# A convolutional transformer block: centre tap as the unit, and no zero padding in the depthwise convolution

## The chip, the cores and the metric

The kernel runs on one core of one Trainium2 chip. The metric is the device time of one execution in microseconds. The kernel before took 4169.58 us, the median of three runs from 4163.44 to 4169.85.

## The reference

The input x has 16 images of 128 channels and 96 x 96 pixels, in float32. One block is computed, cut here to what matters:

```
xn1 = layernorm(x)                       # over the channels of a pixel
x   = x + (attention(xn1 wq, wk, wv) @ wp)   # 8 heads, attention over channels, softmax of 16 x 16
xn2 = layernorm(x)
h1  = w_in . xn2                         # 1x1 projection, 128 -> 512 channels
h2  = depthwise 3x3 conv of h1, padding 1    # one 3x3 filter per channel
x   = x + w_out . gelu(h2)               # 1x1 projection, 512 -> 128 channels
```

The padding is what the change is about: at the image's border a tap of the 3x3 filter meets zeros.

## The kernel before

**Tiles.** The 128 channels lie on the 128 partitions. An image is worked in 8 bands of 12 rows (BR) and a band in 3 units of 4 rows (UR, 384 pixels). There are 128 bands in all. The 512 hidden channels are 4 chunks of 128. TensorE (PE), VectorE (DVE), ScalarE (ACT) and GpSimd (POOL) all work on the convolution; SyncE (SP) issues loads and stores.

**Two ways through the convolution.** Chunks 0 to 2 of every band, and chunk 3 of 62 bands, are "jobs" (conv_job, 446 of them). In a job, PE projects the normalised rows (hidden, L901), ACT copies the result from PSUM into the padded buffer h1s (kept, L906), DVE adds most of the taps (tap, L919: h3 = h1 shifted x ratio + what was there), and ACT makes the products of two or three taps (product, L914), which POOL's accumulating DMAs add up (add_products, L923). Then ACT applies gelu (L927). For chunk 3 of the other 66 bands (by_pe: every second band, which always includes an image's last band, and six of the last eight bands) projection and convolution are one: nine matmuls with composed weights comp, one for each tap, accumulate into one bank (by_matmuls, L969). At the end four matmuls of a unit apply w_out (ffn_out, L992), DVE adds the result to x (L999), and SP stores the band (L1003).

**The unit weight.** The scalar weight of tap 0 is folded into the projection (units, unit_parts), so tap 0 has weight 1. The other taps have the weight divided by it (ratio). DVE's first tap takes the unweighted tap 0 as its second operand, and so does two taps in one instruction.

**Padding.** The rows of the buffers xns (24 rows and two more) and h1s (12 and two more) have WP = 97 columns: one column of zeros serves as the right border of a row and the left border of the next. `window(t, r, n, dx)` is n rows of 96 columns from row r and column dx on. `zeros` fills the border columns of all six xns and four h1s once (L395, L396); `ends` zeroes, for every image, the row above the first and the one below the last (L408). In an image's first band `hidden` projects the zero row above too, in the last band the one below, so that h1s holds zeros there. A job of a later band takes its two upper rows over from the band before (halo, L897), except chunk 3. Chunks of rows are 5, 5, 4 without the halo and 4, 4, 4 with it. So every tap of a job works on 12 x 96 = 1152 elements, and every tap matmul on 384 columns.

**Taps.** Tap t is row t // 3, column t % 3 of the filter; its shift is dy, dx = divmod(t, 3). DMA_TAPS = (1, 2, 3): taps 1 and 2 of each job go over the DMA adds; tap 3 as well for chunk 1. The last job of all has none. DVE has the rest.

**Order.** The instructions' order is written out ahead of time by a planner (class Plan): every step has an engine, a place and dependencies, and an engine always takes the ready step with the smallest place. A place is a job's number plus an offset from the table AT (`at(kind, place)`), with offsets of their own for image 0 (`..._0`). Steps whose offsets differ by more than a few jobs have in effect a fixed rank on their engine.

Of the kernel before, what the change touches and what calls it, by code (L numbers as in the profile page):

```python
# [11 lines left out]
ALU = mybir.AluOpType  # L12
# [5 lines left out]
UR = 4  # L18
BR = 12
# [3 lines left out]
PE_LAST = (0, 1, 2, 4, 5, 7)  # L23
TINY = 1e-20
UNIT_MIN = 1e-18
DMA_TAPS = (1, 2, 3)
THIRD, THIRD_OF, THIRD_CHUNK = (0, 1, 2), 3, 1
PART, Z_PARTS = 24, 6
QT, QB = 4, 1
# [1 line left out]
X1_BUFS, XB_BUFS, PR_BUFS, H3_BUFS, ZT_BUFS = 2, 6, 5, 10, 3  # L31
IN_TURN = ("tr", "h3", "pr", "xb", "x1")
AT = dict(
    load_w=-10.6, weights=-9.25, zeros=-109.85, load_a=-167.55, forth_a=-12.1, stats_a=-7.7, variance_a=338.3,
    power_a=317.55, scaled_a=106.3, gram=-0.45, back_a=-56.1, place_a=121.25, attention=-165.9, mix=-18.8,
    residual=290.95, mixed=-105.85, add_x=-328.55, forth_b=-9.7, stats_b=-262.9, variance_b=95.55,
    power_b=-203.35, shift_b=-87.55, scaled_b=78.75, back_b=0.45, place_b=-79.8, halo=240.1, hidden=4.1,
    kept=-109.5, products=36.25, add_last=-62.55, tap=5.55, add_first=-157.75, gelu=210.35, conv=3.8,
    conv_gelu=5.25, out=7.35, add=0.7, store=226.8, mix_0=-63.1, residual_0=490.65, mixed_0=-265.75,
    add_x_0=-380.65, gram_0=43.45, forth_a_0=-198.65, forth_b_0=-9.45, stats_a_0=-244.4, stats_b_0=-163.95,  # L40
    scaled_a_0=-13.7, scaled_b_0=305.2, back_a_0=-199.3, back_b_0=-62.8, place_a_0=-193.7, place_b_0=23.1,
    shift_b_0=-147.65, late=51.6,
)
STEP = dict(scaled=0.3, hidden=0.1, products=0.5, tap=0.166, conv=1.6, conv_tap=0.03, out=0.8, out_part=0.05)
SLACK = 300
# [164 lines left out]
def tile_restormer_block(  # L210
# [109 lines left out]
    def window(t, r, n, dx=0):  # L320

        return t[:, r * WP + dx : (r + n) * WP + dx].rearrange("p (r w) -> p r w", w=WP)[:, :, :W]

    def part_of(i, r):

        return (i * PARTS + r // PART) % Z_PARTS, r % PART
# [22 lines left out]
    def at(kind, place, i=1):  # L352
        return place + AT[kind if i else kind + "_0"]
# [13 lines left out]
    def t_dve(n):  # L367
        return 100 + 1.067 * n
# [34 lines left out]
    def ends(p, i):  # L403

        for r, at_, u in ((0, 0, -1), (H - 1, PART + 1, UPP)):
            k = part_of(i, r)[0]
            row = window(xns[k], at_, 1, 1)
            op("POOL", 400, at("zeros", p), lambda row=row: nc.gpsimd.memset(row, 0.0), [], [("z", k, u)], 600)  # L408

    def weights(p):  # L410

# [73 lines left out]

        def units():

            w0 = dw[:, :, 0]
            nc.vector.tensor_scalar(unit, w0, -1.0, None, ALU.mult)
            nc.vector.tensor_tensor(unit, unit, w0, ALU.max)  # L490
            nc.vector.tensor_scalar(unit, unit, UNIT_MIN, 3 * UNIT_MIN, ALU.is_lt, ALU.mult)
            nc.vector.tensor_add(unit, unit, w0)
# [390 lines left out]
    def conv_job(j, g, n):  # L883

        i, b = divmod(g, NB)
        kz, r0 = part_of(i, b * BR)
        xn = xns[kz]
        d = {}
        jn = (g, n)
        from_halo = n != PE_CHUNK and b > 0  # L890
        to_halo = n != PE_CHUNK and b < NB - 1
        h1_ = h1s[n]
        step = 4 if from_halo else 5
        chunks = [(k, min(k + step, BR + 2)) for k in range(2 if from_halo else 0, BR + 2, step)]

        def halo():
            nc.scalar.copy(window(h1_, 0, 2, 1), window(h1_, BR, 2, 1))  # L897

        def hidden(r, e):
            ph = d["ph", r] = bank((jn, r), (e - r) * W)  # L900
            nc.tensor.matmul(  # L901
                rows(ph), lhsT=winT[:, n, :], rhs=window(xn, r0 + r, e - r, 1), start=True, stop=True
            )

        def kept(r, e):
            nc.scalar.copy(window(h1_, r, e - r, 1), rows(d.pop(("ph", r))))  # L906

        def shifted(t):
            dy, dx = divmod(t, 3)
            return window(h1_, dy, BR, dx)  # L910

        def product(t):
            to = d["pr", t] = prp.tile([P, BR, W], F32, tag="pr", name=f"pr_{g}_{n}_{t}")
            nc.scalar.activation(to, shifted(t), AF.Copy, scale=ratio[:, n, t : t + 1])  # L914

        def tap(t):
            h3 = h3_of(g, n)
            onto = shifted(0) if t == left[0] else h3
            nc.vector.scalar_tensor_tensor(h3, shifted(t), ratio[:, n, t : t + 1], onto, ALU.mult, ALU.add)  # L919

        def add_products(t):
            to = d["pr", DMA_TAPS[0]] if t != DMA_TAPS[0] else h3_of(g, n)
            nc.gpsimd.dma_start(out=to, in_=d["pr", t], accum_op=ALU.add)  # L923

        def gelu(s0, s1):
            h3 = h3_of(g, n)[:, s0 * UR : s1 * UR, :]
            nc.scalar.activation(h3, h3, AF.Gelu)  # L927

        last = j == len(jobs) - 1
        third = n == THIRD_CHUNK and g % THIRD_OF in THIRD  # L930
        dma_taps = () if last else DMA_TAPS[: 3 if third else 2]
        left = [t for t in range(1, 9) if t not in dma_taps]
        h1 = [("h1", n, k) for k in range(4)]
        h3 = [("h3", jn, s) for s in range(UPB)]
        for k, (r, e) in enumerate(chunks):
            ph = ("h", (jn, r))
            jk, zs = j + STEP["hidden"] * k, z_units(kz, r0 + r, r0 + e)
            to = h1[k + 1 : k + 2] if r else h1[:2]
            pe(t_mm((e - r) * W), at("hidden", jk), lambda r=r, e=e: hidden(r, e), [*zs, ("w", "in")], [ph])
            act(t_copy((e - r) * W), at("kept", jk), lambda r=r, e=e: kept(r, e), [ph], to)  # L940
        for k, t in enumerate(dma_taps):
            jk = j + STEP["products"] * k
            act(t_act(BR * W, 1), at("products", jk), lambda t=t: product(t), h1, [("pr", (jn, t))])
        pr = [("pr", (jn, t)) for t in dma_taps]
        for k, t in enumerate(dma_taps[1:]):
            add(at("add_last", j), lambda t=t: add_products(t), [pr[1 + k]], [pr[0]])
        for k, t in enumerate(left):
            dve(t_dve(BR * W), at("tap", j + STEP["tap"] * k), lambda t=t: tap(t), h1, h3, True)
        if dma_taps:
            add(at("add_first", j), lambda: add_products(DMA_TAPS[0]), [pr[0]], h3)  # L950
        if to_halo:
            act(t_copy(2 * W), at("halo", j), halo, h1[3:], h1[:1])
        for s in range(0, UPB, 1 if last else UPB):
            e = s + 1 if last else UPB
            act(t_act((e - s) * UT), at("gelu", j), lambda s=s, e=e: gelu(s, e), [], h3[s:e])

    def by_matmuls(p, g, s):

        i, b = divmod(g, NB)
        kz, r0 = part_of(i, b * BR + s * UR)  # L960
        xn = xns[kz]
        d = {}
        pc = ("h", (g, PE_CHUNK, s))

        def product(t):
            if t == 0:
                d["pc"] = rows(bank((g, PE_CHUNK, s), UT))
            dy, dx = divmod(t, 3)
            nc.tensor.matmul(  # L969
                d["pc"], lhsT=comp[:, t, :], rhs=window(xn, r0 + dy, UR, dx),  # L970
                start=(t == 0), stop=(t == 8),
            )
# [4 lines left out]
        for t in range(9):  # L977
            dy = t // 3
            zs = z_units(kz, r0 + dy, r0 + dy + UR)
            pe(t_mm(UT), at("conv", p + STEP["conv_tap"] * t), lambda t=t: product(t), [*zs, ("w", "conv")], [pc])  # L980
        act(t_act(UT), at("conv_gelu", p), gelu, [pc], [("h3", (g, PE_CHUNK), s)])

    def ffn_out(p, g, s):
# [49 lines left out]
    for i in range(B):  # L1033
# [44 lines left out]
```

## Time and profile before

| | |
|---|---|
| median of three runs | 4169.58 us |
| the profiled execution | 4165.01 us |
| its span, first to last instruction | 4163.3 us |
| granted TensorE clock, mean | 0.999 |
| PE, DVE, ACT, POOL busy | 99%, 98%, 89%, 59% |
| DMA queues, share of 16 engines | 83.1% and 10.1% |

The busy table gives for each engine its busy time, its share of the span and its number of instructions; PEld is the load of weights, which runs beside PE's matmuls. The chain follows the last instruction back to what released it, and so on to the beginning: the engine that fills it is the one that sets the time. A row of the groups has the line, the engine, the operation, output <- inputs, the shape and the count; after the bar come the busy time, the mean of one in ns, and the idle time ahead of them with what ended it. A row of the timeline has the start, the length and what ran, several in a row merged. A row of the stretches has the stretch, its length, then for PE, PEld, DVE, ACT and POOL the busy time and the number of instructions, the granted clock, the share of the DMA engines and GB/s.

### The profile page before, as it was taken

The page shows a single profiled execution, that of the slowest core. Times are in us where ns is not written, and L with a number is a line of the kernel's source. Part 1 is how long each engine was busy: PE and PEld are TensorE (multiplying, and loading weights), DVE is VectorE, ACT ScalarE, POOL GpSimd, SP SyncE. Part 2 cuts the span into 40 slices and gives each one's busy share as a digit, 9 for nine tenths or more (in the row PEclk, how much of TensorE's full clock was granted, in tenths as well). Part 3 has the DMA queues.
Part 4 walks back from the last instruction along what each step waited for, and adds up shares of the span by engine and source line. Part 5 has one row for each costly group of instructions (what it writes and reads, how often), then busy time and mean ns, then how long its engine had stood idle before and what let it go on. Part 6 is the DMA issues. An engine that isn't in the chain of part 4 may idle for free.

```text
span 4163.3 us, 52440 instructions
## 1 busy us (share of the span) xinstructions
PE 4138.0 (99%) x17457; PEld 2680.2 (64%) x17457; DVE 4072.3 (98%) x4676; ACT 3690.1 (89%) x6971; POOL 2439.2 (59%) x2391
## 2 busy tenths in 40 slices
PE   9999999999999999999999999999999999999999
PEld 7666666666666666666666666666666666666565
DVE  7999999999999999999999999999999999999998
ACT  5999898998999998988988999898898988989885
POOL 4666466565656656566565665556666566565432
PEclk9999999999999999999999999999999999999999
DMA  3999999999999999999999999999999999998997
GB/s 100 197 203 209 193 209 197 213 204 196 217 199 203 201 205 207 199 202 203 202 208 191 212 203 198 214 195 201 205 196 213 199 208 204 202 202 186 200 197 159
DMA packets 203934, 827.63 MB, mean 199 GB/s; under 512 B 23568, under 2 KB 24976, under 8 KB 203664
## 3 DMA queue, kind: packets, MB, share of 16 engines
q0 software_dynamic: 164160, 672.47, 83.1%
q1 hardware_dynamic: 38256, 151.73, 10.1%
q8 instruction: 138, 2.26, 0.2%
q14 instruction: 132, 1.08, 0.1%
q10 hardware_dynamic: 1248, 0.09, 0.0%
HBM read 148.26 MB, written 75.50 MB: 54 GB/s over the span
## 4 chain that ended last, share of the span: by engine, by line
PE 91%; DVE 3%; ACT 3%; DMA 1%; issue 1%; POOL 1%; ACTq 0%; POOLq 0%; DVEq 0%
PE h L969 25%; PE h L992 22%; PE h L901 20%; PE h L568 6%; PE g L679 6%; PE pB_a L716 3%; PE pB_b L716 3%; PE pT_b L611 3%; PE pT_a L611 3%; DVE h L919 2%; DMA h<-pr 1%; ACT pr L914 1%; ACT zT L669 0%; ACT h L906 0%; ACT h L927 0%
## 5 line engine op out<-in xcount | busy, mean ns | idle before, releaser
L919 DVE SCALAR_TENSOR_TENSOR h<-h,ratio,h 128x1152 f32<-128x1152 f32 x2104 | 2913.0, 1405 | 4.2
L914 ACT ACTIVATE pr<-h,ratio 128x1152 f32<-128x1152 f32 x1018 | 1301.5, 1294 | 60.5 <-DMA h<-pr 32.6
L969 PE MATMUL h<-xn,comp 128*128 128x384 f32 x3564 | 1261.5, 486 | 0.0
L992 PE MATMUL h<-h,woutT 128*128 128x384 f32 x3072 | 1132.9, 486 | 0.9 <-ACT h L927 0.3
L901 PE MATMUL h<-xn,winT 128*128 128x384 f32 (+1 forms) x2676 | 1064.7, 500 | 3.7 <-ACT h L906 2.7
L969 PEld LDWEIGHTS h<-xn,comp 128*128 128x128 f32 x3564 | 646.3, 189 | 390.5 <-issue 12.3
L923 POOL DMA_DIRECT2D pr<-pr x573 | 576.0, 1018 | 456.7 <-ACT pr L914 329.0
L906 ACT COPY h<-h 128x384 f32<-128x384 f32 (+1 forms) x1338 | 669.4, 523 | 163.8 <-PE h L901 152.3
L992 PEld LDWEIGHTS h<-h,woutT 128*128 128x128 f32 x3072 | 553.1, 190 | 321.2 <-issue 8.7
L923 POOL DMA_DIRECT2D h<-pr x445 | 415.0, 933 | 500.9 <-DVE h L919 126.6
L901 PEld LDWEIGHTS h<-xn,winT 128*128 128x128 f32 x2676 | 482.4, 190 | 298.7 <-issue 44.0
L919 DVE SCALAR_TENSOR_TENSOR h<-h,ratio 128x1152 f32<-128x1152 f32 x446 | 626.2, 1408 | 14.9 <-ACT h L906 8.4
L927 ACT ACTIVATE h<-h 128x1152 f32<-128x1152 f32 x448 | 538.5, 1208 | 35.0 <-DMA h<-pr 31.7
L629 POOL TENSOR_TENSOR rstd_a<-ve_a,mhalf 128x4 f32<-128x4 f32 x288 | 511.3, 1776 | 11.4 <-POOL ve_a L625 0.2
L629 POOL TENSOR_TENSOR rstd_b<-ve_b,mhalf 128x4 f32<-128x4 f32 x288 | 510.3, 1772 | 9.8
L669 ACT ACTIVATE zT<-pT_b,nb_b,rstd_b 128x128 f32<-128x128 f32 x1132 | 434.9, 497 | 14.8 <-DVE nb_b L633 12.2
L625 POOL TENSOR_SCALAR ve_a<-st_a 128x4 f32<-128x4 f32 x288 | 293.9, 1021 | 230.5 <-DVE st_a L618 199.7
L625 POOL TENSOR_SCALAR ve_b<-st_b 128x4 f32<-128x4 f32 x288 | 269.3, 935 | 257.0 <-DVE st_b L618 231.0
L679 PEld LDWEIGHTS g<-zT 128*128 128x128 f32 x2304 | 293.3, 191 | 44.7 <-issue 2.1
L665 ACT ACTIVATE zT<-pT_a,rstd_a 128x128 f32<-128x128 f32 x1080 | 313.3, 398 | 7.4 <-POOL rstd_a L629 6.4
L679 PE MATMUL g<-zT 128*128 128x129 f32 x2304 | 304.7, 275 | 0.0
L720 ACT ACTIVATE xn<-pB_b,b 128x384 f32<-128x384 f32 x384 | 244.2, 636 | 59.2 <-PE pB_b L716 58.6
(174 smaller groups left out, 3621.5 us busy)
## 6 DMA issues: line engine op xcount, KB each, us to landing
pr<-pr POOLq DMA_DIRECT2D x573, 576.0 KB, 7.3
h<-pr POOLq DMA_DIRECT2D x445, 576.0 KB, 6.8
x<-in_x_dram SPq DMA_DIRECT2D x128, 576.0 KB, 6.3
out_dram<-x SPq DMA_DIRECT2D x127, 576.0 KB, 5.4
x<-in_x_dram POOLq DMA_DIRECT2D x122, 576.0 KB, 7.1
out_dram<-x SPq DMA_DIRECT2D x3, 192.0 KB, 1.9
weights<-in_L_conv_w_in_dram SPq DMA_DIRECT2D x1, 256.0 KB, 3.3
weights<-in_L_conv_w_out_dram SPq DMA_DIRECT2D x1, 256.0 KB, 3.4
```

The source lines that it names most:

```text
L625: nc.gpsimd.tensor_scalar(ve, d["mv"][:, :, 2], 1.0 / C, EPS, ALU.mult, ALU.add)
L629: nc.gpsimd.tensor_tensor(rstd, d["ve"], mhalf, ALU.pow)
L669: nc.scalar.activation(zT(q)[:, k, :P], d["pT", q][:, k, :], AF.Identity, bias=d["nb"][:, t : t + 1], scale=d["rstd"][:, t : t + 1],)
L679: nc.tensor.matmul(grams[i][:, : P + 1], lhsT=zt[:, :P], rhs=zt, start=(q == 0 and k == 0), stop=(q == NU * TPU // QT - 1 and k == QT - 1),)
L901: nc.tensor.matmul(rows(ph), lhsT=winT[:, n, :], rhs=window(xn, r0 + r, e - r, 1), start=True, stop=True)
L906: nc.scalar.copy(window(h1_, r, e - r, 1), rows(d.pop(("ph", r))))
L914: nc.scalar.activation(to, shifted(t), AF.Copy, scale=ratio[:, n, t : t + 1])
L919: nc.vector.scalar_tensor_tensor(h3, shifted(t), ratio[:, n, t : t + 1], onto, ALU.mult, ALU.add)
L923: nc.gpsimd.dma_start(out=to, in_=d["pr", t], accum_op=ALU.add)
L927: nc.scalar.activation(h3, h3, AF.Gelu)
L969: nc.tensor.matmul(d["pc"], lhsT=comp[:, t, :], rhs=window(xn, r0 + dy, UR, dx), start=(t == 0), stop=(t == 8),)
L992: nc.tensor.matmul(rows(d["po"]), lhsT=woutT[:, n, :], rhs=h3s[g, n][:, s * UR : (s + 1) * UR, :], start=(k == 0), stop=(k == NCH - 1),)
```

## The change

The centre tap (4) becomes the unit in place of tap 0. A new helper, `inside`, gives for a tap and some rows the rows and columns that lie inside the image; taps are applied only there. DVE's first tap of a job is now the one below the centre (7), or the one above it (1) in an image's last band: together with the centre it covers every element of the band. The DMA adds take taps 3 and 5, and for chunk 1 also tap 1 (8 in a first band, 0 in a last one), whose rows all lie inside; their products still read the zero columns of h1s. The matmul way begins with the centre tap, which writes the whole bank; the others accumulate into the part that lies inside. First and last bands no longer project the row outside the image. The zeros in xns go, with `ends`; those in h1s stay. Most places of AT are new. The diff, cut to its core, with those places of AT that the prediction speaks of:

```diff
-DMA_TAPS = (1, 2, 3)
+UNIT = 4
+DMA_TAPS = (3, 5)
+FIRST_TAP, THIRD_TAP = 7, 1
+TOP_FIRST, TOP_THIRD = 7, 8
+END_FIRST, END_THIRD = 1, 0
...
 AT = dict(
-    load_a=-167.55, mix=-18.8, add_x=-328.55, power_b=-203.35, scaled_a=106.3, back_b=0.45, place_b=-79.8,
-    hidden=4.1, products=36.25, tap=5.55, conv=3.8, conv_gelu=5.25, out=7.35, add=0.7, store=226.8, ...
+    load_a=-171.6, mix=-35.75, add_x=-284.15, power_b=-306.7, scaled_a=100.7, back_b=-5.05, place_b=36.3,
+    hidden=4.1, products=108.95, tap=5.45, conv=3.9, conv_gelu=5, out=7.4, add=-85.8, store=312.6, ...
...
+    def inside(t, r0, n):
+        dy, dx = divmod(t, 3)
+        cut = slice(max(0, 1 - dx), W - max(0, dx - 1))
+        lo, hi = max(0, 1 - dy - r0), min(n, H + 1 - dy - r0)
+        return lo, hi, cut
...
-        for t, r in [(t, PART + 2) for t in xns[:PARTS]] + [(t, BR + 2) for t in h1s] + [(t, PART + 2) for t in xns[PARTS:]]:
-            op("POOL", 1000, at("zeros", p), lambda t=t, r=r: around(t, r), [], [("w", "in")], 1200)
+        for t in h1s:
+            op("POOL", 1000, at("zeros", p), lambda t=t: around(t, BR + 2), [], [("w", "in")], 1200)
-    def ends(p, i):
...
-            w0 = dw[:, :, 0]
+            wu = dw[:, :, UNIT]
...
-        chunks = [(k, min(k + step, BR + 2)) for k in range(2 if from_halo else 0, BR + 2, step)]
+        row0 = 2 if from_halo else 0 if b else 1
+        row1 = BR + 2 if b < NB - 1 else BR + 1
+        chunks = [(k, min(k + step, row1)) for k in range(row0, row1, step)]
...
         def tap(t):
             h3 = h3_of(g, n)
-            onto = shifted(0) if t == left[0] else h3
-            nc.vector.scalar_tensor_tensor(h3, shifted(t), ratio[:, n, t : t + 1], onto, ALU.mult, ALU.add)
+            if t == left[0]:
+                nc.vector.scalar_tensor_tensor(
+                    h3, shifted(t), ratio[:, n, t : t + 1], shifted(UNIT), ALU.mult, ALU.add
+                )
+                return
+            lo, hi, cut = inside(t, b * BR, BR)
+            to = h3[:, lo:hi, cut]
+            nc.vector.scalar_tensor_tensor(
+                to, shifted(t)[:, lo:hi, cut], ratio[:, n, t : t + 1], to, ALU.mult, ALU.add
+            )
...
-        dma_taps = () if last else DMA_TAPS[: 3 if third else 2]
-        left = [t for t in range(1, 9) if t not in dma_taps]
+        ahead, also = (TOP_FIRST, TOP_THIRD) if b == 0 else (END_FIRST, END_THIRD) if b == NB - 1 else (FIRST_TAP, THIRD_TAP)
+        dma_taps = () if last else (*DMA_TAPS, also) if third else DMA_TAPS
+        left = [ahead, *(t for t in range(9) if t not in (ahead, UNIT, *dma_taps))]
...
+        order = [UNIT, *(t for t in range(9) if t != UNIT)]
...
+            lo, hi, cut = inside(t, b * BR + s * UR, UR)
             dy, dx = divmod(t, 3)
             nc.tensor.matmul(
-                d["pc"], lhsT=comp[:, t, :], rhs=window(xn, r0 + dy, UR, dx),
-                start=(t == 0), stop=(t == 8),
+                d["pc"][:, lo:hi, cut], lhsT=comp[:, t, :], rhs=window(xn, r0 + dy, UR, dx)[:, lo:hi, cut],
+                start=(t == order[0]), stop=(t == order[-1]),
             )
...
-        ends(start2, i)
```

The steps' sizes that the planner reckons with follow the new sizes (tap_size, columns).

More of the change, by code (lines that the diff above doesn't have):

```diff
@@ L33 @@
 AT = dict(
[L34 to L42, printed above, removed]
+    load_w=-0.7, weights=56.25, zeros=-91.75, load_a=-171.6, forth_a=-13.8, stats_a=-13.35, variance_a=472.9,
+    power_a=393.55, scaled_a=100.7, gram=-0.95, back_a=-54.2, place_a=177.7, attention=-168.4, mix=-35.75,
+    residual=220.5, mixed=-116.4, add_x=-284.15, forth_b=-10.05, stats_b=-175.75, variance_b=89.4,
+    power_b=-306.7, shift_b=-89.65, scaled_b=147.3, back_b=-5.05, place_b=36.3, halo=257.25, hidden=4.1,
+    kept=-157.6, products=108.95, add_last=-2.05, tap=5.45, add_first=-115.65, gelu=233, conv=3.9, conv_gelu=5,
+    out=7.4, add=-85.8, store=312.6, mix_0=-83.1, residual_0=398.2, mixed_0=-274.7, add_x_0=-395.85,
+    gram_0=56.85, forth_a_0=-241.65, forth_b_0=-12.45, stats_a_0=-45.05, stats_b_0=-53.25, scaled_a_0=38.7,
+    scaled_b_0=263.2, back_a_0=-243.25, back_b_0=-126.9, place_a_0=-340.95, place_b_0=-9.4, shift_b_0=-42.6,
+    late=7.15,
 )
@@ L399, in zeros @@
             op("POOL", 300, at("zeros", p - 1), lambda t=t: nc.gpsimd.memset(t[:, :, P:], 1.0), [], [("w", "ones")], 500)
-        for t, r in [(t, PART + 2) for t in xns[:PARTS]] + [(t, BR + 2) for t in h1s] + [(t, PART + 2) for t in xns[PARTS:]]:
-            op("POOL", 1000, at("zeros", p), lambda t=t, r=r: around(t, r), [], [("w", "in")], 1200)
-    def ends(p, i):
[L405 to L408, printed above, removed]
+        for t in h1s:
+            op("POOL", 1000, at("zeros", p), lambda t=t: around(t, BR + 2), [], [("w", "in")], 1200)
     def weights(p):
@@ L486, in units @@
         def units():
-            w0 = dw[:, :, 0]
-            nc.vector.tensor_scalar(unit, w0, -1.0, None, ALU.mult)
-            nc.vector.tensor_tensor(unit, unit, w0, ALU.max)
+            wu = dw[:, :, UNIT]
+            nc.vector.tensor_scalar(unit, wu, -1.0, None, ALU.mult)
+            nc.vector.tensor_tensor(unit, unit, wu, ALU.max)
             nc.vector.tensor_scalar(unit, unit, UNIT_MIN, 3 * UNIT_MIN, ALU.is_lt, ALU.mult)
-            nc.vector.tensor_add(unit, unit, w0)
+            nc.vector.tensor_add(unit, unit, wu)
             nc.vector.reciprocal(per_unit, unit)
@@ L917, in tap, with tap_size @@
             h3 = h3_of(g, n)
-            onto = shifted(0) if t == left[0] else h3
-            nc.vector.scalar_tensor_tensor(h3, shifted(t), ratio[:, n, t : t + 1], onto, ALU.mult, ALU.add)
+            if t == left[0]:
[8 more added lines that the diff above has]
+            )
+        def tap_size(t):
+            lo, hi, cut = inside(t, b * BR, BR)
+            return BR * W if t == left[0] else (hi - lo) * (cut.stop - cut.start)
         def add_products(t):
-            to = d["pr", DMA_TAPS[0]] if t != DMA_TAPS[0] else h3_of(g, n)
+            to = d["pr", dma_taps[0]] if t != dma_taps[0] else h3_of(g, n)
             nc.gpsimd.dma_start(out=to, in_=d["pr", t], accum_op=ALU.add)
@@ L937, in conv_job @@
             jk, zs = j + STEP["hidden"] * k, z_units(kz, r0 + r, r0 + e)
-            to = h1[k + 1 : k + 2] if r else h1[:2]
+            to = h1[k + 1 : k + 2] if r > 1 else h1[:2]
             pe(t_mm((e - r) * W), at("hidden", jk), lambda r=r, e=e: hidden(r, e), [*zs, ("w", "in")], [ph])
@@ L947, in conv_job @@
         for k, t in enumerate(left):
-            dve(t_dve(BR * W), at("tap", j + STEP["tap"] * k), lambda t=t: tap(t), h1, h3, True)
+            dve(t_dve(tap_size(t)), at("tap", j + STEP["tap"] * k), lambda t=t: tap(t), h1, h3, True)
         if dma_taps:
-            add(at("add_first", j), lambda: add_products(DMA_TAPS[0]), [pr[0]], h3)
+            add(at("add_first", j), lambda: add_products(dma_taps[0]), [pr[0]], h3)
         if to_halo:
@@ L963, in by_matmuls, with columns @@
         pc = ("h", (g, PE_CHUNK, s))
+        order = [UNIT, *(t for t in range(9) if t != UNIT)]
         def product(t):
-            if t == 0:
+            if t == order[0]:
                 d["pc"] = rows(bank((g, PE_CHUNK, s), UT))
+            lo, hi, cut = inside(t, b * BR + s * UR, UR)
             dy, dx = divmod(t, 3)
             nc.tensor.matmul(
-                d["pc"], lhsT=comp[:, t, :], rhs=window(xn, r0 + dy, UR, dx),
-                start=(t == 0), stop=(t == 8),
-            )
+                d["pc"][:, lo:hi, cut], lhsT=comp[:, t, :], rhs=window(xn, r0 + dy, UR, dx)[:, lo:hi, cut],
+                start=(t == order[0]), stop=(t == order[-1]),
+            )
+        def columns(t):
+            lo, hi, cut = inside(t, b * BR + s * UR, UR)
+            return (hi - lo) * (cut.stop - cut.start)
         def gelu():
             nc.scalar.activation(h3_of(g, PE_CHUNK)[:, s * UR : (s + 1) * UR, :], d["pc"], AF.Gelu)
-        for t in range(9):
+        for k, t in enumerate(order):
             dy = t // 3
             zs = z_units(kz, r0 + dy, r0 + dy + UR)
-            pe(t_mm(UT), at("conv", p + STEP["conv_tap"] * t), lambda t=t: product(t), [*zs, ("w", "conv")], [pc])
+            pe(t_mm(columns(t)), at("conv", p + STEP["conv_tap"] * k), lambda t=t: product(t), [*zs, ("w", "conv")], [pc])
         act(t_act(UT), at("conv_gelu", p), gelu, [pc], [("h3", (g, PE_CHUNK), s)])
```

## The prediction

> **What bounds the kernel now.** I read the page's busy line, then the chain that ended last, then the groups with shapes kept apart, then a few microseconds of TensorE's timeline, then the stretches.
>
> ```profile
> PE 4138.0 (99%) x17457; PEld 2680.2 (64%) x17457; DVE 4072.3 (98%) x4676; ACT 3690.1 (89%) x6971; POOL 2439.2 (59%) x2391
> ...
> PE 91%; DVE 3%; ACT 3%; DMA 1%; issue 1%; POOL 1%; ACTq 0%; POOLq 0%; DVEq 0%
> ```
>
> PE and DVE are both nearly full, and the chain that sets the end runs through PE for 91% of the span. A busy PE may still be a slow PE, so the next rows ask what one matmul costs.
>
> ```profile
> L969 PE MATMUL h<-xn,comp 128*128 128x384 f32 x3564 | 1261.5, 486 | 0.0
> L992 PE MATMUL h<-h,woutT 128*128 128x384 f32 x3072 | 1132.9, 486 | 0.9 <-ACT h L927 0.3
> L901 PE MATMUL h<-xn,winT 128*128 128x384 f32 x2236 | 875.4, 487 | 3.0 <-ACT h L906 2.7 <-ACT x L577 0.2
> L969 PEld LDWEIGHTS h<-xn,comp 128*128 128x128 f32 x3564 | 646.3, 189 | 390.5 <-issue 12.3 <-ACT h L906 0.6 <-ACT xn L722 0.2
> ...
> L901 PE MATMUL h<-xn,winT 128*128 128x480 f32 x440 | 202.6, 566 | 0.7 <-DVE x L999 0.7
> ```
>
> ```profile
> 4127.90 5.97 PE L969 MATMUL h<-xn,comp 128*128 128x384 f32 x18
> ```
>
> One float32 product is two recorded matmuls (3564 = 66 bands x 3 units x 9 taps x 2). In the timeline 18 of them take 5.97 us; without the last one's 0.486 that is 17 steps of 0.3225 us, 0.84 ns a column. The forms of L901 say the same: 96 more columns take 566 - 486 = 80 ns, 0.83 ns each. Step by step from the start times of the trace: 9640 matmuls of 384 columns at 0.3225, 440 of 480 at 0.403, 7175 of 128 or 129 at about 0.110, and some small ones make **4102 us of matmuls that cannot stand closer**. Of the span of 4163 only 61 us is left: 21 in the first 200 us, some 43 spread over 200 to 4000 us (by 200 us stretches: 0.7 at best, 4.7 at worst), almost nothing behind (the steps' rounding makes up the difference). So PE is at its end, and a column taken away is time taken away.
>
> ```profile
> 200.00:1000.00 800.00, 798.86 (x3404) 518.90 (x3403) 792.12 (x910) 729.00 (x1392) 498.65 (x467) 1.00 0.96 204
> 1000.00:2000.00 1000.00, 999.03 (x4236) 647.24 (x4235) 988.28 (x1119) 902.77 (x1713) 602.01 (x575) 1.00 0.96 204
> 2000.00:3000.00 1000.00, 995.23 (x4205) 644.13 (x4204) 985.08 (x1104) 903.78 (x1714) 598.38 (x571) 1.00 0.95 202
> 3000.00:4000.00 1000.00, 999.02 (x4099) 638.68 (x4097) 989.39 (x1104) 900.55 (x1671) 582.88 (x552) 1.00 0.96 202
> ```
>
> The third figure pair is DVE: 1.0 to 1.5% idle in each stretch, hardly more than PE. A saving on one engine alone would soon meet the other. The last columns show the granted clock at 1.00 and the transfers at 96% of their engines, the third nearly full resource.
>
> The Trainium skill, "Perfetto Trace Analysis", section "Identifying the Most-Contended Engine", calls matmul busy time a poor measure and takes the weight loads' busy share; here that is 64%, which by itself would leave PE a third free and make shorter matmuls worth nothing. The steps of 0.3225 us with nothing between them speak against that reading, and I go by them.
>
> **PE, conv products (L969).** With dx of 0 or 2 a tap leaves out one column of 96, 4 of 384: 6 of 9 taps in 66 x 3 = 198 units, 4752 columns. In 17 units (16 last bands and one first band go by matmuls) three taps lose a row as well: 17 x (96 + 95 + 95) = 4862. Together 9614 columns, two matmuls each at 0.84 ns: **16.2 us**.
>
> **PE, projected rows (L901).** The first band of an image no longer computes the row above it, the last not the one below: 63 jobs (16 x 3, and 15 with the fourth chunk) and 48 jobs, 111 rows of 96 columns = 10656 columns x 2 x 0.84: **17.9 us**. The shortest new matmul has 285 columns, 239 ns; the next weights' load of 189 ns still fits behind it, so no load comes to light.
>
> PE together: -34.1 us.
>
> ```profile
> L919 DVE SCALAR_TENSOR_TENSOR h<-h,ratio,h 128x1152 f32<-128x1152 f32 x2104 | 2913.0, 1405 | 4.2
> ...
> L919 DVE SCALAR_TENSOR_TENSOR h<-h,ratio 128x1152 f32<-128x1152 f32 x446 | 626.2, 1408 | 14.9 <-ACT h L906 8.4 <-PE h L992 6.3
> ...
> L633 DVE SCALAR_TENSOR_TENSOR nb_b<-st_b,rstd_b 128x4 f32<-128x4 f32 x288 | 43.4, 151 | 3.6 <-POOL rstd_b L629 3.6
> ```
>
> **DVE taps (L919).** The number stays 2550. Working through the tap lists: 1532 lose 12 elements (12 rows x 95), 222 lose 107 (11 x 95), 111 lose 96 (11 x 96), 685 stay whole; 52794 elements. From the 4 element row to the 1152 element row one element costs (1405 - 151) / 1148 = 1.09 ns: about -57 us. Against it stand gaps: target and second input are now rows of 95 in 96. The x446 row already has a second input with gaps (the h1 window) and takes 3 ns more. Gaps in the target are not in this trace; the bounds are nothing, and 12 rows each as dear as a whole 4 element instruction (12 x 151 = 1812 ns, +0.4 us). I take another 3 ns, by the nearest row: 1754 x 6 = 11 us. **DVE: -46 us.** It is not counted in the sum, since PE gives only 34; it keeps DVE from becoming the bound as long as the gaps cost less than (57 - 34) / 1754 = 13 ns each; beyond that DVE, not PE, limits the gain, and at 32 ns each all of it is gone.
>
> **ACT** copies 111 rows less (L906, 384 to 480 columns: 508 to 601 ns, 0.97 ns each): -10 us, hidden under PE at 89% busy; nothing. **POOL** loses 12 memsets at the start and 32 at image changes (L408: 6.5 us, and 50.6 us of waiting ahead of them, with the adds' issues and the variances queued behind). POOL is 59% busy and 1% of the chain: nothing, at best a few us. **Transfers**: the same 1018 adds of 576 KB (taps 3 and 5 instead of 2 and 1), 83.1% + 10.1% of 4163 = 3880 us, which still fits. The weights' preparation has as many instructions as before.
>
> **The new order.** The places tell which step goes first on an engine. On PE only mix (-18.8 to -35.8) and back_b (0.45 to -5.05) move noticeably; the order hidden, conv, out stays. On ACT products go behind scaled_a and place_b behind conv_gelu; on POOL power_b comes ahead of add_x, so the adds to x, with their transfers, wait one power of 1.8 us longer, and what is late then is the residual's band, six buffers deep; on DVE add moves far ahead of the taps; on SP load_a stays ahead of store. No step gains a wait. I cannot see the new instruction order, so I bound it by the stretches of this trace: all as good as the best (0.7 us per 200) would be -30 us, all as bad as the worst (4.7) +46. I take 0, since PE's list hardly changes.
>
> **Sum.** The profiled execution: span 4163.3, with what lies around it 4165.0. 4165.0 - 34.1 = 4130.9. The three runs shown (4163.4, 4169.6, 4169.9) average 2.6 above that execution: **4133**.
>
> **Rivals.**
> *The order gives the gain back.* PE's idle time from 200 to 4000 us grows from 43 to 77 us, 4.1 in each stretch, a value that the worst stretch exceeds: 4133 + 34 = 4167, no change. For it: DVE is as full as PE, so small shifts show. Against: DVE loses more work than PE, so there is more play than before. 0.08; worse than the worst stretch (above 4178): 0.03.
> *Rows with gaps slow TensorE's writes: slower than before.* 2376 matmuls (1188 products) now write runs of 95 into rows of 96; no matmul of the trace writes with a gap. Bounds: nothing, or each of four rows as dear as a 128 column matmul, 4 x 109 - 322 = +114 ns, which makes 4133 + 271 = 4404. It decides from 14 ns each (34 us / 2376), and from 18 ns the kernel is slower by over 0.2%. I take nothing: reading with gaps costs nothing (L969 reads rows of 96 in 97 and L992 without gaps, both 486). 0.08.
> The Trainium skill, "PSUM — Partial Sum Buffer", section "Specifications (TRN2)", says that any non-contiguous pattern slows matmuls significantly; it gives no figure, and no row here has such a write. Taken at its word it would put this rival first.
> *The conv does not follow its columns* (a run of 95 costs as much as 96 and rows as much as before): only the projected rows' 17.9 us come, 4149. 0.05.
> *The order gets better than the best stretch*: below 4103. 0.04.
>
> **Numbers.** The forecast holds 0.72. Range: 4133 - 30 to 4133 + 45, 4103 to 4178; it leaves out 0.04 below and 0.11 above. 0.2% of 4169.6 is 8.3 us, about what a measurement can tell from no change. Faster: 0.72 + 0.04 + 0.05 = 0.81; same 0.08; slower 0.08 + 0.03 = 0.11.
>
> **What would show it.** L969 in four forms (2308 of 380 columns stepping at 0.319 us, 1154 of 384, 34 of 288, 68 of 285); L901 with 222 of 288 columns and 2014 of 384; L919's large group near 2870 us; the chain again 90% PE. I am wrong if steps of 380 columns are longer than those of 384, if the summed matmul steps fall by 34 us but the span does not (the order), or if DVE's idle time vanishes while PE's grows.

## The result, and the profile after

The changed kernel takes 4158.07 us (median of 20 runs, 4153.48 to 4163.76) beside 4167.22 us for the kernel before (20 runs, 4163.44 to 4171.64). The ratio is 0.9977, interval 0.997 to 0.9984: faster by 0.23%, some 9 us, where 34 were forecast. The time lies within the stated range of 4103 to 4178; the gain is smaller than forecast by a factor of nearly four. Of the later runs, one execution each of e7 and e10 took 10351 and 13388 us; these two slow ones count in their medians but not in their ratios.

The page of the changed kernel, busy line and chain:

```profile
PE 4116.1 (99%) x17457; PEld 2679.0 (64%) x17457; DVE 4023.1 (97%) x4676; ACT 3673.4 (88%) x6971; POOL 2466.3 (59%) x2347
...
PE 84%; ACT 7%; DVE 5%; DMA 2%; issue 1%; POOL 1%; POOLq 0%; ACTq 0%; DVEq 0%
```

PE's share of the chain fell from 91% to 84%, and ACT, DVE and the transfers took its place: the end is now set more often by what PE waits for. The groups with shapes kept apart tell whether the matmuls became shorter (count, then busy us, mean ns):

```profile
L991 PE MATMUL h<-xn,comp 128*128 128x380 f32 x2308 | 866.3, 482 | 0.0
L907 PE MATMUL h<-xn,winT 128*128 128x384 f32 x2014 | 787.4, 487 | 3.9 <-ACT h L912 2.5 <-ACT xn L724 0.9 <-ACT x L581 0.6
...
L991 PE MATMUL h<-xn,comp 128*128 128x384 f32 x1154 | 467.4, 486 | 4.3 <-ACT h L912 3.9 <-ACT x L581 0.4
...
L907 PE MATMUL h<-xn,winT 128*128 128x288 f32 x222 | 72.0, 406 | 0.0
...
L991 PE MATMUL h<-xn,comp 128*128 128x285 f32 x68 | 21.8, 402 | 0.0
```

They did, and each form has the count that was forecast. A line of TensorE's timeline shows the step:

```profile
1204.58 5.93 PE L991 MATMUL h<-xn,comp 128*128 128x384 f32 x18
```

(5.93 - 0.486) / 17 = 0.3202 us where it was 0.3225; by the start times of the trace the 380 column matmuls step at 0.319 us and those of 384 at 0.3225. Summed up, the matmuls that cannot stand closer fell from 4102.1 to 4068.1 us: **the 34.0 us of work are gone.** But the span fell only by 7.1, from 4163.3 to 4156.2. What lies between the matmuls grew from 61 to 88 us. Most of it is in the main part: the idle time seen in the start times from 200 to 4000 us grew from 43 to 67 us, in the first 200 from 21 to 23. The stretches, columns as before:

```profile
1000.00:2000.00 1000.00, 994.30 (x4254) 649.02 (x4252) 975.64 (x1114) 903.59 (x1724) 615.18 (x570) 1.00 0.96 204
2000.00:3000.00 1000.00, 994.14 (x4222) 646.71 (x4220) 976.64 (x1115) 900.75 (x1714) 616.17 (x567) 1.00 0.96 203
3000.00:4000.00 1000.00, 992.82 (x4085) 637.10 (x4084) 972.82 (x1099) 892.79 (x1671) 579.16 (x541) 1.00 0.96 201
```

DVE is idle 2.3 to 2.7% of the main part now, PE stands still longer, and the clock and the transfers' 96% are as before. DVE did not take over as the bound. PE's waits say who did. Each row has the waiting instruction, the releaser, us in all, times, and the longest. First the kernel before, then the changed one:

```profile
PEld h L992 <- ACT h L927: 5.0, 10, 0.9
...
PE h L901 <- ACT h L906: 2.7, 1, 2.7
...
PE h L992 <- ACT h L927: 0.3, 1, 0.3
```

```profile
PEld h L1018 <- ACT h L945: 17.9, 26, 1.3
PEld h L572 <- ACT h L912: 8.6, 9, 2.0
...
PE h L1018 <- ACT h L945: 4.9, 14, 0.7
PE h L572 <- ACT h L912: 4.1, 4, 1.4
PE h L991 <- ACT h L912: 3.9, 1, 3.9
...
PE h L907 <- ACT h L912: 2.9, 2, 2.5
...
PE h L1018 <- ACT h L912: 1.1, 2, 0.9
```

The output matmuls (L1018) wait 22.8 us for gelu (L945), against 5.3 us, when the rows of PE and PEld are added. That sum is a mark of a late gelu and not time lost: a weight load can wait while PE still runs the matmul ahead of it. By PE's own rows gelu costs 4.9 us (0.3 before), and the waits for the copies of the projection (L912, before L906) grow more, from 2.9 to 12.0 us. The longest single stall behind the start is one of these. It is seen in ScalarE's timeline, whose bracket gives the idle time ahead of the instruction and what ended it:

```profile
3509.96 1.15 ACT L945 ACTIVATE h<-h 128x1152 f32<-128x1152 f32 x1
3516.02 1.26 ACT L920 ACTIVATE pr<-h,ratio 128x1152 f32<-128x1152 f32 x1 [4.91 <-DMA h<-pr]
3517.18 1.15 ACT L945 ACTIVATE h<-h 128x1152 f32<-128x1152 f32 x1
3518.23 0.46 ACT L912 COPY h<-h 128x384 f32<-128x384 f32 x1
```

A product waits 4.9 us for one of the five product buffers, which an adding transfer still reads (the chain has it at 8.84 us, against a median of 7.1). Everything behind it in ACT's order waits too: a gelu, the copy that frees a bank, and so the matmul at 3518.74, which has stood 3.9 us.

So there were two suspects at the outset: the new order (late gelus and late copies), and transfers that are too near their limit for a faster PE.

### The profile page after: what moved, and what is told of

It is laid out like the page before. It is cut to its first block, busy times and chain, and to the rows that moved or that the text cites. A ratio compares the mean times of both kernels' runs of the same rounds, so it can differ in the third digit from the quotient of the medians.

```text
span 4156.2 us, 52372 instructions
## 1 busy us (share of the span) xinstructions
PE 4116.1 (99%) x17457; PEld 2679.0 (64%) x17457; DVE 4023.1 (97%) x4676; ACT 3673.4 (88%) x6971; POOL 2466.3 (59%) x2347
## 3 DMA queue, kind: packets, MB, share of 16 engines
q0 software_dynamic: 164160, 672.47, 83.4%
q1 hardware_dynamic: 38256, 151.73, 10.2%
## 4 chain that ended last, share of the span: by engine, by line
PE 84%; ACT 7%; DVE 5%; DMA 2%; issue 1%; POOL 1%; POOLq 0%; ACTq 0%; DVEq 0%
PE h L991 22%; PE h L1018 21%; PE h L907 18%; PE g L683 5%; PE h L572 5%; DVE h L931 3%; PE pB_a L720 3%; PE pT_b L615 3%; PE pT_a L615 2%; PE pB_b L720 2%; ACT pr L920 2%; DMA pr<-pr 1%; ACT zT L673 1%; DMA h<-pr 1%; ACT h L912 1%
## 5 line engine op out<-in xcount | busy, mean ns | idle before, releaser
L931 DVE SCALAR_TENSOR_TENSOR h<-h,ratio,h 128x1140 f32<-128x1140 f32 (+2 forms) x2104 | 2856.9, 1379 | 5.3
L920 ACT ACTIVATE pr<-h,ratio 128x1152 f32<-128x1152 f32 x1018 | 1310.4, 1295 | 69.1 <-DMA h<-pr 41.1
L991 PE MATMUL h<-xn,comp 128*128 128x380 f32 (+1 forms) x3564 | 1261.9, 481 | 4.3 <-ACT h L912 3.9
L1018 PE MATMUL h<-h,woutT 128*128 128x384 f32 x3072 | 1134.1, 488 | 6.2 <-ACT h L945 4.9
L907 PE MATMUL h<-xn,winT 128*128 128x384 f32 (+1 forms) x2676 | 1045.3, 494 | 4.3 <-ACT h L912 2.9
L941 POOL DMA_DIRECT2D pr<-pr x573 | 557.9, 988 | 507.5 <-ACT pr L920 332.2
L912 ACT COPY h<-h 128x384 f32<-128x384 f32 (+1 forms) x1338 | 652.1, 513 | 187.4 <-PE h L907 175.5
L1018 PEld LDWEIGHTS h<-h,woutT 128*128 128x128 f32 x3072 | 555.3, 190 | 335.6 <-ACT h L945 17.9
L941 POOL DMA_DIRECT2D h<-pr x445 | 428.8, 966 | 469.2 <-PE h L907 66.6
L907 PEld LDWEIGHTS h<-xn,winT 128*128 128x128 f32 x2676 | 481.6, 190 | 292.5 <-issue 42.2
L945 ACT ACTIVATE h<-h 128x1152 f32<-128x1152 f32 x448 | 537.3, 1203 | 12.3 <-DMA h<-pr 9.2
L633 POOL TENSOR_TENSOR rstd_b<-ve_b,mhalf 128x4 f32<-128x4 f32 x288 | 496.0, 1723 | 12.2
L629 POOL TENSOR_SCALAR ve_b<-st_b 128x4 f32<-128x4 f32 x288 | 290.1, 1007 | 269.0 <-DVE st_b L622 259.5
L629 POOL TENSOR_SCALAR ve_a<-st_a 128x4 f32<-128x4 f32 x288 | 305.4, 1061 | 241.7 <-DVE st_a L622 213.8
L572 PE MATMUL h<-xn,mwT 128*128 128x384 f32 x768 | 287.1, 489 | 5.2 <-ACT h L912 4.1
```

The source lines that it names most:

```text
L629: nc.gpsimd.tensor_scalar(ve, d["mv"][:, :, 2], 1.0 / C, EPS, ALU.mult, ALU.add)
L633: nc.gpsimd.tensor_tensor(rstd, d["ve"], mhalf, ALU.pow)
L907: nc.tensor.matmul(rows(ph), lhsT=winT[:, n, :], rhs=window(xn, r0 + r, e - r, 1), start=True, stop=True)
L931: nc.vector.scalar_tensor_tensor(to, shifted(t)[:, lo:hi, cut], ratio[:, n, t : t + 1], to, ALU.mult, ALU.add)
L991: nc.tensor.matmul(d["pc"][:, lo:hi, cut], lhsT=comp[:, t, :], rhs=window(xn, r0 + dy, UR, dx)[:, lo:hi, cut], start=(t == order[0]), stop ...
L1018: nc.tensor.matmul(rows(d["po"]), lhsT=woutT[:, n, :], rhs=h3s[g, n][:, s * UR : (s + 1) * UR, :], start=(k == 0), stop=(k == NCH - 1),)
```

## The experiments

All kernels ran with the kernel before beside them on the same chip, so the ratio carries the comparison; its median beside them was 4165.1 to 4167.9 us, so times from different rows are good to some 2 us only. "Between" is the span of the profiled execution less the summed matmul steps (4068.1 us with the new work, 4102.1 with the old); "gelu" is the output matmuls' wait for it, PE and PEld together, so a mark and not a loss. Old and new places mean the tables AT of the two kernels.

| run | what it is | us | ratio to before, interval | between | gelu |
|---|---|---|---|---|---|
| before | old work, old places | 4167.22 | 1 | 61 | 5.3 |
| after | new work, new places | 4158.07 | 0.9977, 0.997 to 0.9984 | 88 | 22.8 |
| e1 | new work, exactly the old order | 4145.63 | 0.9952, 0.994 to 0.9965 | 76 | 7.7 |
| e2 | old work, exactly the new order | 4193.12 | 1.0066, 1.0054 to 1.0079 | 86 | 18.7 |
| e3 | after, transfers halved | 4144.19 | 0.9947, 0.9934 to 0.9961 | 73 | 19.9 |
| e4 | before, transfers halved | 4154.01 | 0.9972, 0.996 to 0.9983 | 49 | 5.3 |
| e5 | e1, transfers halved | 4126.12 | 0.9901, 0.9886 to 0.9916 | 57 | 5.9 |
| e8 | e1, VectorE's taps whole | 4154.89 | 0.9969, 0.9956 to 0.9981 | 85 | 7.5 |
| e7 | after, old places | 4138.97 | 0.9936, 0.9922 to 0.9949 | 66 | 10.5 |
| e12 | e7, allowance 340 | 4133.15 | 0.9917, 0.9903 to 0.993 | 64 | 4.3 |
| f5 | e7, allowance 260 | 4136.86 | 0.9931, 0.9915 to 0.9948 | 67 | 3.2 |
| e11 | after, allowance 340 | 4142.45 | 0.994, 0.9928 to 0.9953 | 73 | 21.8 |
| e10 | before, new places | 4186.95 | 1.0047, 1.0033 to 1.0061 | 82 | 27.1 |
| e6 | after, ScalarE's places old | 4148.30 | 0.9954, 0.9942 to 0.9967 | 79 | 23.0 |
| e9 | after, GpSimd's places old | 4144.68 | 0.9945, 0.9932 to 0.9957 | 72 | 25.6 |
| f2 | after, both of these old | 4147.53 | 0.9959, 0.9944 to 0.9974 | 77 | 19.5 |
| f3 | after, all other places old | 4134.16 | 0.9925, 0.9911 to 0.994 | 64 | 4.6 |
| f1 | after, output matmuls 0.2 jobs later | 4162.81 | 0.9995, 0.9986 to 1.0005 | 92 | 24.4 |
| g1 | after, TensorE's places old | 4141.70 | 0.9934, 0.9919 to 0.9949 | 68 | 6.3 |
| g2 | after, VectorE's places old | 4161.53 | 0.9986, 0.9976 to 0.9995 | 90 | 21.4 |

### Order and work, crossed (e1, e2)

e1 issues the changed kernel's instructions in the order of the kernel before, instruction for instruction on every engine: it has the old table and the old zeroing (zeros, ends), the planner reckons with the old sizes, and only what is issued is cut.

```diff
-        chunks = [(k, min(k + step, row1)) for k in range(row0, row1, step)]
+        chunks = [(k, min(k + step, BR + 2)) for k in range(2 if from_halo else 0, BR + 2, step)]
+        def issued(r, e):
+            return max(r, row0), min(e, row1)
...
-            dve(t_dve(tap_size(t)), ...
+            dve(t_dve(BR * W), ...
```

> The instructions of the changed kernel (cut taps, cut rows, centre tap) in exactly the order of the kernel before, with its zeroing of the buffers kept. Theory O, the new order costs what the work saves: without the new order the saving of 34 us shows, 4167 - 34 = about 4133. Theory T, the transfers are too near their limit for any order: 4150 to 4160, TensorE's idle time up by some 25 us as in the changed kernel. Theory S, an order fits the sizes it was reckoned for: also no better than 4155, but with the idle time on waits that have no late transfer behind them.

e2 is the reverse: the new order exactly, with every tap, conv product and projected row whole (28 more memsets at the very start fill the borders once).

```diff
+    def whole(n):
+        return 0, n, slice(0, W)
...
+        def issued(r, e):
+            return (10, 14) if e - r == 3 else (r, e)
...
-            lo, hi, cut = inside(t, b * BR, BR)
+            lo, hi, cut = whole(BR)
...
-            lo, hi, cut = inside(t, b * BR + s * UR, UR)
+            lo, hi, cut = whole(UR)
```

> The order of the changed kernel with the work of the kernel before: full taps, full conv products, 14 rows projected in the border bands (border rows of the image come out different, since the rows outside are not zeroed anew). Theory O: TensorE has its 34 us back and the new order's stalls stay, 4158 + 34 = about 4192. Theory T: the transfers get back the time that they lack, TensorE's idle time falls to near that of the kernel before, 4165 to 4175.

In their traces PE, DVE and ACT run the same instructions in the same sequence as in the kernel before (e1) and in the changed one (e2). Measured: e1 0.9952, 20 us less than before, between the two expectations. e2 1.0066, 27 us more than before; theory O had said 25, and theory T is out as the whole cause. Read across the table: with the old work the new order costs 27 us, with the new work 10 to 12 (4158 against 4145.6). Read down: the new work saves 35 us in the new order (4193 to 4158), all that was forecast, and 20 in the old one. The column "between" says the same: in the new order the stalls stay (86 and 88 us), and all of the work comes off; in the old order they grow from 61 to 76. So of the 25 us that are missing, 10 to 12 go with the new order as against the exact old one, and some 14 are missing in the old order too, which was reckoned for the old sizes. Why its stalls grow is answered only in part, by the transfers (next section).

### The transfers (e3, e4, e5)

```diff
-            nc.gpsimd.dma_start(out=to, in_=d["pr", t], accum_op=ALU.add)
+            nc.gpsimd.dma_start(out=to[:, : BR // 2], in_=d["pr", t][:, : BR // 2], accum_op=ALU.add)
```

> The changed kernel, but each accumulating transfer adds only the first 6 of 12 rows (the lower half of the products is left out of the result); number and order of all instructions as in the changed kernel. Theory T: with the transfers far from their limit TensorE's idle time falls from 90 us in the profile to under 55, 4158 - 35 = about 4123 or less. Theory O with stalls that are no matter of the transfers: within 8 us of 4158.

> The kernel before with the same halved transfers. It has 43 us of TensorE's idle time in the main part, most of it in pieces of 50 to 150 ns that come with changes of tile. Theory T and theory O alike: little to win, 4155 to 4165; below 4150 would say that the transfers cost the kernel before as well.

> The old order with the new work, and each accumulating transfer adding only 6 of 12 rows (half of the products is left out). If what is missing of the 34 us in the old order (it gave 20) is transfers that come late, the whole saving shows against the kernel before with halved transfers: 4154 - 34 = about 4120, TensorE's idle time in the main part near 31 us. If it is missing because the order does not fit the new sizes, transfers or not: 4154 - 20 = about 4134.

The change takes hold, as the page of e3 shows (KB of one, us to landing), where it was 7.5 and 7.1 us:

```profile
pr<-pr POOLq DMA_DIRECT2D x573, 288.0 KB, 4.1
h<-pr POOLq DMA_DIRECT2D x445, 288.0 KB, 3.8
```

The changed kernel gains 14 us from it, not the 35 that theory T wanted, and not the under 8 of theory O either. The kernel before gains 12 on the kernel beside it (4165.6), a little more than expected, though 4154 is not below the 4150 that was named as the sign; e5 gains 20 on e1. So halving the adds is worth 12 to 20 us in all three versions tried: the transfers are a tax on this kernel that the prediction left in the base. They do not explain the missing gain. With halved transfers on both sides the change is worth 10 us (4154.0 to 4144.2), with whole ones 9. The rows of ScalarE say so too: its products (L914, L920) and gelus (L927, L945) stood 88 us for transfers in the kernel before and 75 in the changed one, so not longer. First the rows of the kernel before, then those of the changed kernel, then its products with halved transfers:

```profile
L914 ACT ACTIVATE pr<-h,ratio 128x1152 f32<-128x1152 f32 x1018 | 1301.5, 1294 | 60.5 <-DMA h<-pr 32.6 <-DMA pr<-pr 23.5
...
L927 ACT ACTIVATE h<-h 128x1152 f32<-128x1152 f32 x445 | 537.1, 1213 | 31.7 <-DMA h<-pr 31.7
```

```profile
L920 ACT ACTIVATE pr<-h,ratio 128x1152 f32<-128x1152 f32 x1018 | 1310.4, 1295 | 69.1 <-DMA h<-pr 41.1 <-DMA pr<-pr 24.4
...
L945 ACT ACTIVATE h<-h 128x1152 f32<-128x1152 f32 x445 | 536.0, 1208 | 9.5 <-DMA h<-pr 9.2
```

```profile
L920 ACT ACTIVATE pr<-h,ratio 128x1152 f32<-128x1152 f32 x1018 | 1308.8, 1295 | 6.5 <-DMA h<-pr 3.7
```

Nor do the transfers make the late gelus: those waits stay at 19.9 us in e3, with transfers that land 3 us sooner. What falls in e3 is PE's wait for the copies, from 12.0 to 5.4 us. In the old order, however, the transfers do take a part: with halved transfers the new work is worth 28 us (4154.0 to 4126.1), with whole ones 20; the last 6 us stay open.

### VectorE's share (e8)

e8 is e1 with whole taps, so that only PE's part of the work is cut.

> The old order, TensorE's part cut (conv products and projected rows) but VectorE's taps whole again (border rows of the image then take in stale rows). By the sum, in which TensorE alone decides, 4146 stays. If VectorE, 98% busy, is a bound beside it, most of the 20 us goes: 4155 to 4165.

Measured 0.9969: 4155, 13 us less than before, and 7 to 9 of the 20 us are gone. The chains of e1 and of e8:

```profile
PE 87%; DMA 4%; DVE 4%; ACT 4%; issue 1%; POOL 1%; ACTq 0%; POOLq 0%; DVEq 0%
```

```profile
PE 80%; DVE 10%; ACT 5%; DMA 4%; issue 1%; POOL 1%; ACTq 0%; POOLq 0%; DVEq 0%
```

With DVE's work left whole its share of the chain rises from 4% to 10%, and the gain in the old order falls from 20 us to 13. So the cut taps are worth 7 to 9 us of the gain, although PE alone was counted. The two ran on different chips and their intervals touch (0.994 to 0.9965, 0.9956 to 0.9981), so the size is rough.

### Places or draw (e7, e10, e11, e12, f5)

e7 is the changed kernel with the whole old table, e10 the kernel before with the whole new one. In e11, e12 and f5 the planner's allowance for a result to reach another engine is changed, which gives other orders from the same places.

```diff
-SLACK = 300
+SLACK = 340
```

> The changed kernel with the whole table of places of the kernel before; unlike the run with the old order exactly, the planner reckons with the new sizes. If it is the places that are worse: near 4146, like the old order. If an order reckoned with the new sizes is better suited to them: 4130 to 4140. If every new order is a new draw whatever the places: anywhere from 4135 to 4165.

> The kernel before with the new table of places and nothing else changed; the planner makes the order for the old sizes. If the new places are worse in themselves: 4167 + 19 = about 4186 (19 is what they cost with the new work). If a table only suits the work it was made beside, likewise above 4180, so this run does not tell these two apart; if the new places are as good as the old ones and the changed kernel's order was a poor draw: 4160 to 4175.

> The changed kernel, with the planner's allowance for a result to reach another engine 340 instead of 300 ns: the same places, another order. If the new places are worse: again 4150 to 4165. If the order of the changed kernel was a poor draw among many: near 4140.

> The changed kernel with all places of the kernel before and the allowance of 340 instead of 300: again another order. If the old places are better: 4133 to 4146, as with 300 (4139). If 4139 was a good draw: 4150 to 4165.

> The changed kernel with all places of the kernel before and the planner's allowance at 260 ns: a third order from the old table. With 300 it took 4139, with 340 4133. If the table is what counts: 4130 to 4146. If single orders scatter more than the tables differ: outside that.

With the old places the changed kernel takes 4139, 4133 and 4137 us in three orders: 27 to 35 us less than before by the ratios. e12, at 4133.15, is the fastest kernel here that does the whole work. With the new places it takes 4158 and 4142. So a single order is worth some 6 us of scatter among the old places and 16 between the two orders from the new ones; in each pair with the same allowance the new places are slower, by 17 us (0.9977 against 0.9936) and 10 us (0.994 against 0.9917), and with the old work by 20 (e10). The new table is worse in itself, and the order of the changed kernel is the poorer of the two drawn from it. What e11 saves is not gelu's wait, which stays at 21.8 us, but PE's wait for the copies (L912), 3.1 us where it was 12.0. e7 is 7 us better than e1, which would say that old places serve the cut work better when the planner knows the new sizes; single orders differ as much, so that is not shown.

### Whose places (e6, e9, f1, f2, f3, g1, g2)

Each takes the changed kernel and puts the places of some engines back to the old table, image 0's included; as an example the core of g1, with the unchanged places between these and image 0's left out:

```diff
-    ... forth_a=-13.8, ... gram=-0.95, back_a=-54.2, ... mix=-35.75, ... forth_b=-10.05, ... back_b=-5.05, ... conv=3.9, ... out=7.4, ...
+    ... forth_a=-12.1, ... gram=-0.45, back_a=-56.1, ... mix=-18.8, ... forth_b=-9.7, ... back_b=0.45, ... conv=3.8, ... out=7.35, ...
```

> The changed kernel with ScalarE's places alone (products, scaled, place, kept, mixed, gelu, halo) as in the kernel before; the planner makes a new order from them. If the products' lower rank behind scaled_a, and with it later adds and later gelus, is what the new order costs: 4158 - 12 = 4146 or less, and the output matmuls' waits for gelu fall from 23 us to under 10. If the cost is elsewhere in the order: 4153 to 4165.

> The changed kernel with GpSimd's places alone (the adds, add_x, variance, power, zeros) as in the kernel before. If power_b ahead of add_x and the adds' lower rank make the transfers start late: 4158 - 8 = 4150 or less, and the output matmuls' waits for gelu (23 us) fall to about 10, as with all places back. If those waits come with ScalarE's and GpSimd's places together or with neither: 4153 to 4163.

> The changed kernel with ScalarE's and GpSimd's places together as in the kernel before, all others new. If these two carry the whole cost: 4139, gelu waits near 10 us. If they are half of it or less: 4146 to 4158.

> The complement: TensorE's, VectorE's, SyncE's and the weights' places as in the kernel before, ScalarE's and GpSimd's new. If ScalarE's and GpSimd's places carry the cost: 4150 to 4162, gelu waits near 20 us. If the others do: near 4139, gelu waits under 10 us.

> The changed kernel with TensorE's places alone as in the kernel before (mix, back_b, forth, gram, conv, out; hidden is the same in both). If TensorE's order carries the cost: 4132 to 4142, waits for gelu under 10 us. If it does not: 4150 to 4162 with 19 us or more of them.

> The changed kernel with VectorE's places alone as in the kernel before (add, stats, shift, residual, tap). If VectorE's order carries the cost (its add ahead of everything, its statistics): 4132 to 4142, waits for gelu under 10 us. If it does not: 4150 to 4162 with 19 us or more. If neither this nor TensorE's alone does it, it is the two together, or loads and stores.

And f1, which moves the output matmuls alone (out=7.4 to 7.6):

> The changed kernel with one place changed: the output matmuls at 7.6 instead of 7.4 jobs, a fifth of a job (some 2 us) later. If the new places cost time because gelu comes too late for the output matmuls, their waits for it fall from 23 us to under 10 and the time to 4140 to 4147. If those waits are only where a general lateness shows, they go elsewhere: 4150 to 4165.

ScalarE's and GpSimd's old places bring 10 to 13 us each, but together no more (0.9959), and the waits for gelu stay at 19.5 to 25.6 us: these gains are no larger than the 16 us by which two orders of one table differ, so they cannot be told from a draw. Their complement f3 brings all of it, 0.9925, with ScalarE's and GpSimd's places still new. Of f3's engines VectorE's places do nothing that passes the scatter (0.9986), TensorE's do it alone: g1 0.9934, like e7's 0.9936. One such run proves little, since g1 and e11 (0.994, TensorE's places new) cannot be told apart. The whole set does: the five orders of the changed kernel with TensorE's old places (e7, e12, f5, f3, g1) gain 27 to 35 us, the seven with its new ones (after, e11, e6, e9, f2, f1, g2) 2 to 25. The waits for gelu part the same way, 3.2 to 10.5 us against 19.5 to 25.6; the row of g1 that answers to the 17.9 us of the changed kernel, and the same row of e11:

```profile
PEld h L1010 <- ACT h L937: 4.6, 8, 1.8
```

```profile
PEld h L1018 <- ACT h L945: 16.5, 23, 1.5
```

That these two runs take the same time, 4142 us, with waits for gelu of 6.3 and 21.8 us, shows again that the wait is not lost one for one.

The traces also show what TensorE's places do to its list. Count for each matmul how many matmuls of the projection (L901, in the changed kernel L907) PE ran ahead of it. In the changed kernel that number differs from the kernel before for 36% of the conv products and 28% of the output matmuls; with TensorE's places put back (g1) for none and 4%.

f1 failed as a cure: 4163 us, waits 24.4 us. Starting the output matmuls later neither removes the wait nor wins time; since the wait stayed, f1 does not tell what its removal would be worth. Which of TensorE's places it is (conv and out moved by 0.1 and 0.05 jobs, gram by 0.5, forth_a by 1.7, back_a by 1.9, back_b by 5.5, mix by 17) was not taken apart.

## Why the prediction was wrong, point by point

**What bounds the kernel: right.** PE's matmul steps fill the span but for 49 to 92 us in every version. But PE does not set the time alone: with VectorE's taps left whole (e8) 7 to 9 us of the gain are gone, and halved transfers bring 12 to 20 us.

**PE's work: right.** 34.1 forecast, 34.0 measured (4102.1 to 4068.1), in the forecast forms and counts. e2 against the changed kernel shows these columns worth 35 us while the weight loads were busy for 64% of the span. The Trainium skill, "Perfetto Trace Analysis", section "Identifying the Most-Contended Engine", judges TensorE's headroom by MFU (the share of peak FLOP/s) and the weight loads' busy share, not by matmul busy time; here that second share by itself misses that TensorE was nearly full.

**Writes with gaps: right to take nothing.** The 2308 matmuls that write runs of 95 into rows of 96 step at 0.319 us, which is 0.84 ns a column as without gaps. The Trainium skill, "PSUM — Partial Sum Buffer", section "Specifications (TRN2)", says any non-contiguous pattern slows matmuls significantly; this pattern (one element left out in 96) did not, and the measurement decides.

**DVE: right in kind, mis-sized in the safe direction.** The rows of the changed kernel:

```profile
L931 DVE SCALAR_TENSOR_TENSOR h<-h,ratio,h 128x1140 f32<-128x1140 f32 x1532 | 2104.6, 1393 | 3.4
...
L931 DVE SCALAR_TENSOR_TENSOR h<-h,ratio,h 128x1045 f32<-128x1045 f32 x222 | 285.0, 1293 | 0.4
...
L931 DVE SCALAR_TENSOR_TENSOR h<-h,ratio,h 128x1056 f32<-128x1056 f32 x111 | 144.5, 1305 | 0.4
```

12 elements less take 1405 - 1393 = 12 ns less, 107 elements 112 ns, both with gaps in the target; 96 elements less in whole rows, without gaps, take 100 ns less. All three are 1.0 to 1.05 ns an element, so the gaps cost nothing. The group (all forms together) fell from 2913.0 to 2856.9, by 56 us instead of 46. That DVE must fall with PE was argued; e8 shows it, with some 7 to 9 us.

**The new order: the step that failed.** It read: "I take 0, since PE's list hardly changes". Both halves failed. PE's list does change: the prediction held that "the order hidden, conv, out stays", and 36% of the conv products and 28% of the output matmuls stand behind another number of projections than before. And the change costs: with PE's old places the gain is 27 to 35 us in five orders (g1, which puts back nothing else, 27), with its new ones 2 to 25 in seven, and the changed kernel, at 9, is among the poorer of these. The places were weighed by their size, and a shift of 0.05 or 0.1 jobs was passed over, while PE has 1% of play in which such a shift must find room. Nor was it weighed how good the old order was. Of all versions with whole transfers only the five with PE's old places and the new work come near its 43 us between the matmuls from 200 to 4000 us, or a few us below; all others lie some 6 us above or more. So there was much to lose and little to gain. The price of the order was -30 to +46 by its bounds and came out at +24 (43 to 67 us). Not all of it is the list's: the exact old order with the new work (e1) stands 15 us longer than the kernel before over the whole span (61 to 76). How the new sequence on PE makes the copies and gelus late was not followed further and stays open.

**The rival that was closest** was "the order gives the gain back", with idle time growing from 43 to 77 us in the main part; it grew to 67, and 4158 lies between the forecast of 4133 and its 4167. It had 0.08, which was too little; its "DVE is as full as PE, so small shifts show" was the better argument. The prediction also named the sign that came: "if the summed matmul steps fall by 34 us but the span does not (the order)".

**Transfers: "still fits" was right for the sum, not for the moment.** Their share (83.4% + 10.2%) left room on average, but some adds land late: 17% of them took over 9 us in the kernel before and 21% in the changed one, where the median is 7, and ScalarE, which works in a fixed order, stood 88 and 75 us for them. Halving them is worth 12 to 20 us in the three versions tried. They are no part of the difference between the two orders, and take some 8 us of the new work's worth in the old order.

The forecast time, 4133, is what the same work takes with the old places and the allowance of 340 (4133.15): the sum was a sum for the work alone. That the two agree so closely is luck, since three orders from that table lie between 4133 and 4139.

## What to carry to other kernels

On a kernel whose busiest engine has 1 to 2% of play, price the work and the order apart. The work, columns times the step, came out here within a microsecond (34.1 and 34.0); the order took back 25 of these 34 us, and no order made here was much better than the old one. Cross the two (old order with new work, new order with old work) before judging an edit that changes both; here that shows a gain of 34 us behind one of 9. Draw several orders before blaming a place: two orders from one table differed by 16 us. And a long wait in the profile shows where a poor order is felt; pushing the waiting step later (f1) did not help.

## What the runs showed of the hardware that was not expected

An output pattern of 95 columns in rows of 96 is free on TensorE (0.319 us for 380 columns, 0.3225 for 384 without gaps) and on VectorE (1.0 to 1.05 ns for each element left out, with gaps or without); only its cost was uncertain beforehand, and it is nothing. Transfers that are 93 to 94% busy over the span take their share of the time though they are 1 to 4% of the chain: halving the adds shortened their landing from about 7 to about 4 us and the kernels by 0.28 to 0.5%.
